# Layer 0's row maxima: turned in fp32, and split into three bfloat16 parts behind the turn on ScalarE and GpSimd instead of ahead of it on VectorE

## The chip, the cores and the metric

The kernel runs on one core of a Trainium2 chip, in one launch. The metric is device time in microseconds. The engines are called as the profile calls them: PE (TensorE matmul), PEld (TensorE weight load), DVE (VectorE), ACT (ScalarE), POOL (GpSimd) and SP (the queue that issues most DMAs). Each engine works through its own instructions in order and waits on semaphores for the others.

## The reference

Two layers work on an input of 2 x 1024 tokens with 256 features. Each normalises its input and adds the results of an attention and of a feed-forward network. Layer 0's attention, where the change lies, is causal, has 32 heads of 8 features and 8 key heads, and is computed in fp32:

```python
scores = jnp.einsum('bhqd,bhkd->bhqk', q, k_rep) / scale
scores = jnp.where((kpos > qpos)[None, None], -jnp.inf, scores)
attn = jax.nn.softmax(scores, axis=-1)
out = jnp.einsum('bhqk,bhkd->bhqd', attn, v_rep)
return out.transpose(0, 2, 1, 3).reshape(B, T, C) @ Wo + bo
```

Its feed-forward network has weights and activations rounded to float8; layer 1 has an attention with another reshape and a feed-forward network with ternary weights. They matter here only as neighbours on the same engines.

## The kernel before

**Tiles.** Layer 0's attention goes through 16 query tiles of 128 tokens, (batch, tile) = (0,0) to (0,7) and then (1,7) down to (1,0). Below they are called turns 0 to 15, since each has one turn of its maxima. Queries and keys are kept as three bfloat16 parts each, stacked along the partitions of the tiles qmain, qlast, kmain and klast, so that a sum of bfloat16 products gives scores of nearly fp32 accuracy.

**The maxima.** For a tile, max_unit (line 1000) computes the scores with the queries along the partitions from the first parts alone (L1012), adds the causal mask (L984), and DVE reduces them to the negated maximum over the keys (L1024) into the tile mx: 128 queries x 32 heads in fp32. For tiles with i > 3 the keys are taken in two halves, and take_max joins the two results by a minimum.

**The turn.** The exponentials are computed with the keys along the partitions and the queries along the free dimension, so -max can't be an activation's bias. It goes into the matmul: three extra rows of qlast hold -max as three bfloat16 parts, and the matching rows of klast hold ones. For this, take_max (line 1032) splits mx by four DVE instructions (L1039 to L1042): a cast, a subtraction, a cast and a subtraction. Three slots later turn_max (line 1045) transposes all three parts, 96 columns, in one bfloat16 transposition on PE (L1047). ACT copies the result from PSUM (L1049), a DMA writes it to DRAM (L1051), and two DMAs bring it into the rows of qlast (L1053).

**The weighing.** weigh (line 1071) computes scores of 128 keys x 4 heads x 128 queries by two matmuls each (L1076: s<-qmain, then s<-qlast, which adds the low parts and -max). ACT takes the exponential (L1086), POOL zeroes what the mask forbids on the diagonal (L1090), and gather (L1106) adds p times v into acc, one group of four p later. Scores and turned maxima share a PSUM pool of four buffers (ps_t); the maxima have three of their own (ps_s).

**The order.** PE's order is written by hand. A slot holds one pair of score tiles, some maxima of later tiles (at a rate that spreads their cost), and a piece of other work: the float8 feed-forward network (ffn0, L268 to L318), the ternary weights of layer 1 (on DVE L342 to L350, on POOL the four products L351 to L354, then a DMA L339), layer norms (L184 to L205), projections and the splitting of their results (L824 to L829), normalising and output (L1121 to L1150). A function handed to after(n, f) runs n slots later. A tile's weighing begins 10 slots after its maxima are done (6 for the first three). The order on the other engines is made by a scheduler when the program is built; it does not follow the source line by line, so that an added instruction can also move its neighbours.

**Queues.** The three DMAs of a turn stand on SP's queue among the loads of later queries (L936), keys (L894) and inputs (L62). POOL's queue holds the diagonal selects, additions into x (L281, L1149, L1150), the ternary products, and DMA issues of its own.

Of the kernel before, what the change touches and what calls it, by code (L numbers as in the profile page):

```python
# [10 lines left out]
F32 = mybir.dt.float32  # L11
BF = mybir.dt.bfloat16
# [4 lines left out]
ALU = mybir.AluOpType  # L17
# [3 lines left out]
P = 128  # L21
# [6 lines left out]
NH0, KV0, HD0 = 32, 8, 8  # L28
# [21 lines left out]
def two_layers(ctx: ExitStack, tc: tile.TileContext, a: dict, out: bass.AP):  # L50
    nc = tc.nc
# [16 lines left out]
    ident = cp.tile([P, P], F32, tag="ident", name="ident")  # L68
    make_identity(nc, ident)
    ident_bf = cp.tile([P, P], BF, tag="ident_bf", name="ident_bf")  # L70
# [4 lines left out]
    for name, op, fill, sign in (  # L75
# [3 lines left out]
        m = both[name] = zp.tile([P, 2, P], BF, tag=name, name=name)  # L79
        nc.gpsimd.memset(m, 0.0)  # L80
        for e in range(2):
            for t in range(2):
                part = m[HALF * e : HALF * e + HALF, t, :]
                nc.gpsimd.affine_select(
                    out=part,
                    in_=part,
# [705 lines left out]
    def attention0(w, qlast, tables):  # L792
# [11 lines left out]
        with ExitStack() as es:  # L804
            pool = es.enter_context(tc.tile_pool(name="a0", bufs=2))
            es.enter_context(tc.manual_schedule(engines={mybir.EngineType.PE}))
            dram = es.enter_context(tc.tile_pool(name="a0d", bufs=2, space=bass.MemoryType.DRAM))
            ps_s = es.enter_context(tc.tile_pool(name="a0s", bufs=3, space=PSUM))
            ps_t = es.enter_context(tc.tile_pool(name="a0t", bufs=4, space=PSUM))
# [155 lines left out]
            def after(slots, f):  # L965
                later.append((slot + slots, f))
# [65 lines left out]
            def take_max(b, i):  # L1032
                both = mx.pop((b, i))
                m = both[:, 0].rearrange("p e n -> p (e n)")
                parts = pool.tile([P, 3, NH0], BF, tag="mparts", name=f"mp{b}{i}", bufs=1)
                r = pool.tile([P, NH0], F32, tag="mrest", name=f"mr{b}{i}")
                if i > 3:
                    nc.vector.tensor_tensor(both[:, 0], both[:, 0], both[:, 1], ALU.min)
                nc.vector.tensor_copy(parts[:, 0], m)  # L1039
                nc.vector.tensor_tensor(r, m, parts[:, 0], ALU.subtract)  # L1040
                nc.vector.tensor_copy(parts[:, 1], r)
                nc.vector.tensor_tensor(parts[:, 2], r, parts[:, 1], ALU.subtract)  # L1042
                after(3, lambda: turn_max(b, i, parts))

            def turn_max(b, i, parts):
                ps = ps_t.tile([P, P], BF, tag="t", name=f"mt{b}{i}")
                nc.tensor.transpose(ps[: 3 * NH0], parts.rearrange("p a h -> p (a h)"), ident_bf)  # L1047
                mt = pool.tile([3 * NH0, P], BF, tag="mt", name=f"mts{b}{i}", bufs=2)
                nc.scalar.copy(mt, ps[: 3 * NH0])  # L1049
                scr = dram.tile([3 * NH0, P], BF, tag="mscr", name=f"mscr{b}{i}")  # L1050
                nc.sync.dma_start(out=scr, in_=mt)  # L1051
                for e in range(2):
                    nc.sync.dma_start(  # L1053
                        out=qst[b, i][1][HALF * e + AUG : HALF * e + AUG + 3],
                        in_=scr.rearrange("(a e n) t -> e a n t", a=3, e=2)[e],
                    )

            def max_units(b, i):

                if i > 3:  # L1060
                    for p in range(16):
                        yield 1024, lambda p=p: max_unit(b, i, [p], 0, 512, 1, False)
                lo = 512 * (i // 4)
                width = (i % 4 + 1) * P
                n = (4, 2, 1, 1)[i % 4]
                for p in range(0, 16, n):
                    yield 2 * n * width, lambda p=p: max_unit(b, i, list(range(p, p + n)), lo, width, 0, True)
                yield 0, lambda: take_max(b, i)
# [375 lines left out]
```

## Time and profile before

| | |
|---|---|
| three timed runs | 1151.48, 1151.53, 1152.94 us; median 1151.53 |
| the profiled execution | 1152.2 us, its span 1150.4 us |
| mean granted PE clock | 0.927 |
| layer 0 (from the chain's lines) | to about 770 us |
| L1024, all reductions to maxima | 608 instructions, 373.0 us of DVE |
| L1086, all exponentials of layer 0 | 576 instructions, 307.6 us of ACT |
| L1090, diagonal selects | 128 instructions, 83.0 us of POOL |
| the turns (L1047 on PE) | 16, from 64.2 to 738.9 us |

The profile shows one execution. In its lists of groups, a row is a line of the kernel, an engine, an operation, the tile written and those read, the shapes and the number of instructions; behind the bar stand the busy time in all and the mean duration of one in ns; behind a second bar, how long the engine was idle just before, and who ended that. In the timeline a row begins with its start and its length in us. In the chain of waits each piece is followed back to what released it; shares are of the span.

### The profile page before, as it was taken

The page shows a single profiled execution, that of the slowest core. Times are in us where ns is not written, and L with a number is a line of the kernel's source. Part 1 is how long each engine was busy: PE and PEld are TensorE (multiplying, and loading weights), DVE is VectorE, ACT ScalarE, POOL GpSimd, SP SyncE. Part 2 cuts the span into 40 slices and gives each one's busy share as a digit, 9 for nine tenths or more (in the row PEclk, how much of TensorE's full clock was granted, in tenths as well). Part 3 has the DMA queues.
Part 4 walks back from the last instruction along what each step waited for, and adds up shares of the span by engine and source line. Part 5 has one row for each costly group of instructions (what it writes and reads, how often), then busy time and mean ns, then how long its engine had stood idle before and what let it go on. Part 6 is the DMA issues. An engine that isn't in the chain of part 4 may idle for free.

```text
span 1150.4 us, 19967 instructions
## 1 busy us (share of the span) xinstructions
PE 1008.0 (88%) x7676; PEld 483.0 (42%) x7699; DVE 761.3 (66%) x1434; ACT 607.9 (53%) x1097; POOL 400.4 (35%) x440
## 2 busy tenths in 40 slices
PE   5858797897998989998989989987999999898897
PEld 2333332232432313232323333334567677576576
DVE  6567977889687898889796879413554544543531
ACT  3014571674455757688867766852564444433431
POOL 2007224324135121412123254554744535413400
PEclk9758896998899989999999999998899999989998
DMA  5432101101102010100010110008522332331100
GB/s 176 120 103 75 53 2 40 21 21 41 55 3 51 6 28 10 37 10 8 21 24 5 28 26 6 5 7 103 86 49 47 79 58 43 82 63 34 39 20 20
DMA packets 65927, 49.04 MB, mean 43 GB/s; under 512 B 20904, under 2 KB 59432, under 8 KB 65832
## 3 DMA queue, kind: packets, MB, share of 16 engines
q1 hardware_dynamic: 60632, 39.05, 15.0%
q0 software_dynamic: 4112, 8.26, 3.0%
q8 instruction: 60, 0.98, 0.4%
q10 hardware_dynamic: 1088, 0.46, 0.1%
q14 instruction: 35, 0.29, 0.1%
HBM read 34.12 MB, written 15.20 MB: 43 GB/s over the span
## 4 chain that ended last, share of the span: by engine, by line
PE 53%; DVE 25%; DMA 8%; ACT 6%; POOL 3%; issue 3%; SPq 2%; DVEq 0%; ACTq 0%; POOLq 0%
DVE mx L1024 13%; PE acc L1106 8%; PE s L1076 7%; PE f1gu L672 5%; PE sk L551 4%; PE f1o L711 3%; PE m L1012 3%; PE pqk L465 3%; PE sq L516 3%; DMA qscr<-ptq 2%; PE gu L301 2%; ACT p L1086 2%; DMA qs<-mscr 2%; SPq L936 2%; DMA qkv<-all 2%
## 5 line engine op out<-in xcount | busy, mean ns | idle before, releaser
L1024 DVE TENSOR_REDUCE mx<-m 128x1 f32<-128x512 f32 (+3 forms) x608 | 373.0, 653 | 99.8 <-PE m L1012 53.3
L1086 ACT ACTIVATE p<-s 128x512 f32<-128x512 f32 x576 | 307.6, 606 | 123.1 <-PE s L1076 119.1
L1106 PE MATMUL acc<-p,v 128*9 128x512 f32 x1152 | 170.4, 610 | 1.8 <-ACT p L1086 1.2
L1090 POOL TENSOR_SCALAR_AFFINE_SELECT p<-p 128x512 f32<-128x512 f32 x128 | 83.0, 673 | 152.6 <-ACT p L1086 152.4
L1012 PE MATMUL m<-k,qmain 64*128 64x512 bf16 (+3 forms) x384 | 95.1, 357 | 43.7 <-DVE mx L1024 34.4
L1012 PE MATMUL m<-kmain,qmain 64*128 64x512 bf16 (+3 forms) x384 | 81.7, 330 | 21.8 <-DVE mx L1024 19.9
L1012 PEld LDWEIGHTS <-qmain 64*128 64x128 bf16 x768 | 50.3, 98 | 80.9 <-issue 52.0
L984 PEld LDWEIGHTS <-ident_h 64*128 64x128 bf16 x832 | 45.7, 97 | 82.7 <-issue 59.8
L984 PE MATMUL m<-mask_q,ident_h 64*128 64x128 bf16 (+3 forms) x832 | 73.7, 221 | 1.8 <-DVE mx L1024 1.7
L1076 PE MATMUL s<-qmain,k 64*128 64x512 bf16 x288 | 65.7, 394 | 6.3 <-DVE att L1129 2.7
L1076 PE MATMUL s<-qmain,kmain 64*128 64x512 bf16 x288 | 65.3, 385 | 6.7 <-ACT p L1086 4.2
L1076 PE MATMUL s<-qlast,k 35*128 35x512 bf16 x288 | 62.8, 390 | 0.0
L1076 PE MATMUL s<-qlast,klast 35*128 35x512 bf16 x288 | 61.5, 381 | 0.0
L1076 PEld LDWEIGHTS <-k 64*128 64x128 bf16 (+1 forms) x576 | 21.0, 95 | 93.0 <-issue 84.5
L672 PEld LDWEIGHTS <-wgu_bf 128*128 128x128 bf16 x384 | 38.5, 101 | 42.4 <-issue 6.8
L681 DVE SCALAR_TENSOR_TENSOR h<-h,f1gu 128x512 f32<-128x512 f32 x32 | 22.0, 686 | 51.6 <-ACT h L680 51.6
L686 POOL TENSOR_TENSOR sq<-h 128x512 f32<-128x512 f32 x28 | 29.1, 1040 | 70.3 <-DVE h L682 67.5
L551 PE MATMUL sk<-qs,ks 25*128 25x128 f32 x512 | 45.3, 424 | 7.7 <-DMA qs<-mscr 7.6
L1149 POOL TENSOR_TENSOR x<-x,aos 128x256 f32<-128x256 f32 x16 | 12.6, 788 | 112.6 <-ACT aos L1148 112.6
L559 ACT ACTIVATE p<-sk 128x2048 f32<-128x2048 f32 x16 | 30.0, 1878 | 41.0 <-PE sk L551 41.0
L524 DVE TENSOR_REDUCE m<-sq 128x16 f32<-128x2048 f32 x16 | 36.6, 2287 | 21.8 <-PE sq L516 21.7
L154 POOL TENSOR_TENSOR hp<-hrest,hp 128x512 bf16<-128x512 f32 x32 | 37.0, 1157 | 34.8 <-ACT hp L153 34.8
(288 smaller groups left out, 1803.1 us busy)
## 6 DMA issues: line engine op xcount, KB each, us to landing
qmain<-qscr SPq DMA_DIRECT2D x64, 96.0 KB
qkv<-all SPq DMA_DIRECT2D x16, 384.0 KB
qscr<-ptq POOLq DMA_DIRECT2D x6, 384.0 KB, 4.2
x<-in_x SPq DMA_DIRECT2D x16, 128.0 KB
qmain<-qscr SPq DMA_DIRECT2D x32, 64.0 KB
qs<-qkv SPq DMA_DIRECT2D x16, 128.0 KB
ks<-qkv SPq DMA_DIRECT2D x16, 128.0 KB
vs<-qkv SPq DMA_DIRECT2D x16, 128.0 KB
```

Source lines behind the costliest of these rows:

```text
L154: engines[1].tensor_tensor(parts[2], r, parts[1], ALU.subtract)
L465: nc.tensor.matmul(pqk, x[k], wqk[:, k, :], start=(k == 0), stop=(k == 1))
L524: last(nc.vector.tensor_reduce(m, ps, AX.X, ALU.max, negate=True))
L551: nc.tensor.matmul(ps[:, s, r, :], columns(k, slice(S * s, S * s + HD + 9), 4 * b + r), columns(q, slice(S * s, S * s + HD + 9), 4 * b + r ...
L672: nc.tensor.matmul(ps[g], wgu_bf[:, k, g * HID + hc * P : g * HID + (hc + 1) * P], x_parts[n][m][:, k, :], start=(k == 0 and m == 0), stop ...
L984: nc.tensor.matmul(out[e][:, :, lo:], ident_h[rows, t, :], rhs.to_broadcast([HALF, out[e].shape[1], P - lo]), start=start and t == 0, stop ...
L1012: nc.tensor.matmul(sc[e][:, s * width : (s + 1) * width], qst[b, i][0][rows, p, :], kst[b][0][rows, lo // 512, p // 4, 0:width], start=not ...
L1024: reduced = nc.vector.tensor_reduce(mx[b, i][:, part, e, pairs[0] : pairs[0] + n], sc[e][:, : n * width].rearrange("p (s k) -> p s k", s=n ...
L1076: nc.tensor.matmul(sc[e], kst[b][n][rows, j // 4, u, j % 4 * P : (j % 4 + 1) * P], qst[b, i][n][rows, 4 * u : 4 * u + 4, :], start=n == 0, ...
L1086: nc.scalar.activation(p, sc[e], AF.Exp, scale=scale)
L1090: nc.gpsimd.affine_select(out=by_head, in_=by_head, compare_op=ALU.is_ge, fill=0.0, base=0, pattern=[[0, 4], [1, P]], channel_multiplier=-1,)
L1106: nc.tensor.matmul(acc[32 * s : 32 * s + HD0 + 1, :], vst[b][:, j, 4 * G + s, :], ps[s], start=(j == 0), stop=(j == i),)
```

## The change

take_max keeps the fp32 maxima and no longer splits them; for i > 3 it still joins the two halves on DVE. turn_max transposes the 32 fp32 columns on PE into an fp32 PSUM tile. Behind it ACT copies the result twice from PSUM, once as bfloat16 (the first part) and once as fp32; POOL subtracts the one from the other; ACT casts the rest to bfloat16 (the second part); POOL subtracts again and writes the third part. Then come the same three DMAs, of a tile of 32 partitions x 3 x 128 instead of 96 partitions x 128. The tile mt has one buffer where it had two, and the new tiles turned and rest have one each.

```diff
             def take_max(b, i):
                 both = mx.pop((b, i))
                 m = both[:, 0].rearrange("p e n -> p (e n)")
-                parts = pool.tile([P, 3, NH0], BF, tag="mparts", name=f"mp{b}{i}", bufs=1)
-                r = pool.tile([P, NH0], F32, tag="mrest", name=f"mr{b}{i}")
                 if i > 3:
                     nc.vector.tensor_tensor(both[:, 0], both[:, 0], both[:, 1], ALU.min)
-                nc.vector.tensor_copy(parts[:, 0], m)
-                nc.vector.tensor_tensor(r, m, parts[:, 0], ALU.subtract)
-                nc.vector.tensor_copy(parts[:, 1], r)
-                nc.vector.tensor_tensor(parts[:, 2], r, parts[:, 1], ALU.subtract)
-                after(3, lambda: turn_max(b, i, parts))
-
-            def turn_max(b, i, parts):
-                ps = ps_t.tile([P, P], BF, tag="t", name=f"mt{b}{i}")
-                nc.tensor.transpose(ps[: 3 * NH0], parts.rearrange("p a h -> p (a h)"), ident_bf)
-                mt = pool.tile([3 * NH0, P], BF, tag="mt", name=f"mts{b}{i}", bufs=2)
-                nc.scalar.copy(mt, ps[: 3 * NH0])
-                scr = dram.tile([3 * NH0, P], BF, tag="mscr", name=f"mscr{b}{i}")
-                nc.sync.dma_start(out=scr, in_=mt)
+                after(3, lambda: turn_max(b, i, m))
+
+            def turn_max(b, i, m):
+
+                ps = ps_t.tile([P, P], F32, tag="t", name=f"mt{b}{i}")
+                nc.tensor.transpose(ps[:NH0], m, ident)
+                turned, rest = (
+                    pool.tile([NH0, P], F32, tag=f"m{x}", name=f"m{x}{b}{i}", bufs=1) for x in ("turned", "rest")
+                )
+                mt = pool.tile([NH0, 3, P], BF, tag="mt", name=f"mts{b}{i}", bufs=1)
+                nc.scalar.copy(mt[:, 0], ps[:NH0])
+                nc.scalar.copy(turned, ps[:NH0])
+                nc.gpsimd.tensor_tensor(rest, turned, mt[:, 0], ALU.subtract)
+                nc.scalar.copy(mt[:, 1], rest)
+                nc.gpsimd.tensor_tensor(mt[:, 2], rest, mt[:, 1], ALU.subtract)
+                scr = dram.tile([3, NH0, P], BF, tag="mscr", name=f"mscr{b}{i}")
+                nc.sync.dma_start(out=scr.rearrange("a n t -> n a t"), in_=mt)
                 for e in range(2):
                     nc.sync.dma_start(
                         out=qst[b, i][1][HALF * e + AUG : HALF * e + AUG + 3],
-                        in_=scr.rearrange("(a e n) t -> e a n t", a=3, e=2)[e],
+                        in_=scr[:, 16 * e : 16 * e + 16],
                     )
```

In the new kernel the transposition is L1042, the three copies are L1047, L1048 and L1050, the two subtractions L1049 and L1051, and the DMAs L1053 and L1055.

As the programs are built, PE's order is the same but for the transposition. DVE has 64 rows fewer, ACT 32 more and POOL 32 more. On ACT the first two copies stand where the one copy stood. What stands between the second and the third copy on ACT, and just ahead of the first subtraction on POOL, is, by the lines of the kernel before:

| turn | on ACT between second and third copy | on POOL ahead of the first subtraction |
|---|---|---|
| 1 | L824 | L864 |
| 3 | two L1086 | L352 |
| 4 | L1115 | L351 |
| 5 | L824 | L864 |
| 6 | three L1086 | L353 |
| 7, 8, 15 | one L1086 | L1090; L354; L1150 |
| 9 | nothing | L351 |
| 10 | L313 | L1090 |
| 13 | L1115 | L1150 |
| 14 | one L198 | L354 |
| 0, 2, 11, 12 | nothing | L242; L1090 in 2, 11 and 12 |

In turn 1 POOL's second diagonal select comes behind L829 where it came ahead of it; in turns 3 and 7 some selects come behind ternary products; in turn 5 two exponentials come ahead of the cast L828 on ACT, and L829 comes behind L353 on POOL.

## Prediction

> **What bounds the kernel now.** I read the page first, then the table by stage, the groups by form, the chain of waits in order of time, and last the timeline around each of the 16 places where a maximum is turned. The profiled execution took 1152.2 us (span 1150.4 us and 1.8 us around it); the three timed runs have a median of 1151.53 us. My sum is made against 1152.2 and moved by -0.67 at the end.
>
> ```profile
> PE 1008.0 (88%) x7676; PEld 483.0 (42%) x7699; DVE 761.3 (66%) x1434; ACT 607.9 (53%) x1097; POOL 400.4 (35%) x440
> ...
> PE 53%; DVE 25%; DMA 8%; ACT 6%; POOL 3%; issue 3%; SPq 2%; DVEq 0%; ACTq 0%; POOLq 0%
> ```
>
> The first line says that PE is the busiest; the second, of the chain that ended last, that a quarter of the span hangs on DVE and little on ACT or POOL. By stage, 100 to 700 us has DVE busy 38 to 45 us of each 50 and PE 41 to 47, ACT 18 to 43, POOL 9 to 20: there layer 0's maxima (L1024) and scores take turns as the bound.
>
> ```profile
> L1049 ACT COPY mts<-mt 96x128 bf16<-96x128 bf16 x16 | 4.2, 265 | 5.8 <-PE mt L1047 5.8
> L1047 PE MATMUL mt<-ident_bf,mp 128*96 128x128 bf16 x16 | 4.0, 250 | 1.5 <-ACT p L1086 0.9 <-DVE v L957 0.6
> L1039 DVE CAST mp<-mx 128x32 bf16<-128x32 f32 x16 | 3.3, 206 | 0.1
> L1041 DVE CAST mp<-mr 128x32 bf16<-128x32 f32 x16 | 3.2, 201 | 0.2
> L1042 DVE TENSOR_TENSOR mp<-mr,mp 128x32 bf16<-128x32 f32 x16 | 3.2, 201 | 0.2
> L1040 DVE TENSOR_TENSOR mr<-mx,mp 128x32 f32<-128x32 f32 x16 | 2.9, 183 | 0.2
> ```
>
> These are all the rows that the change takes away: after the bar, busy us in all and mean ns of one.
>
> **What DVE gains.** 206 + 201 + 201 + 183 = 791 ns a turn, 12.7 us in all, but not all of it is on the path. The chain in order of time holds 3.9 us of these four lines (turns 2, 3, 4, 5, 10, 11, 12, 13). Two of its pieces:
>
> ```profile
> 161.20 0.63 DVE mp L1039
> ...
> 162.89 0.10 DVE mr L1040
> ```
>
> I count **-3.9**. The remaining 8.8 us stand beside PE work and I take them as nothing; if DVE is second in line in those places too, up to that much more could come off.
>
> **What ACT and POOL get.** One copy of 265 ns becomes three, of 32x128. The trace has none of that shape; 128 elements a partition took 265 ns here, 128x256 took 371 ns (L1148), a 128x4 activation 0.21 us: I take 0.26, the row with the same free size, so +0.52 us a turn. The two POOL subtractions, 32x128, stand between a 128x8 iota (154 ns) and 128x256 (672 ns, L281); the straight line through 672 and 1157 ns (128x512, L825) gives 0.43 us, which I take. Handing on from ACT to POOL and back costs 0.08 and 0.03 us (at 271.83 and 271.18 us). So a turn's parts take at least 0.52 + 0.08 + 0.43 + 0.03 + 0.26 + 0.08 + 0.43, about 1.8 us instead of 0.26, on two queues that others share.
>
> The new wait is the price: **the third copy (L1050 of the new kernel) waits on ACT for POOL's first subtraction, and the exponentials behind it wait too.** The order of the built programs tells what stands ahead of that subtraction on POOL. In turns 2, 3, 7, 10, 11 and 12 POOL is free, or ACT has a gap behind the copy (1.76 us at 131.05, 22.4 us at 195.41, 1.68 us at 671.48): nothing. In four turns POOL is in the middle of a ternary weight's L351 to L354. Turn 8:
>
> ```profile
> 473.39 1.16 POOL L351 TENSOR_TENSOR tmg<-tmg,tlg 128x512 bf16<-128x512 bf16 x1 [2.06 <-DVE tlg L350]
> ...
> 474.06 0.26 ACT L1049 COPY mts<-mt 96x128 bf16<-96x128 bf16 x1
> ...
> 475.03 2.07 ACT L1086 ACTIVATE p<-s 128x512 f32<-128x512 f32 x4 [0.70 <-PE s L1076]
> ...
> 477.28 1.05 PE L1106 MATMUL acc<-p,v 128*9 128x512 f32 x8
> 478.11 1.15 POOL L354 TENSOR_TENSOR wgu_bf<-tmg,twg 128x512 bf16<-128x512 bf16 x1
> ```
>
> The new order has the subtraction behind L354, which ends at 479.26; the third copy stands behind the first of the four exponentials. It can run at 479.7, so the second exponential starts at 479.9 instead of 475.53, the gather (477.28) gets its last operand at 480.5 and PE goes on at 480.9 instead of 478.25: **+2.7**. By the same reading:
> - Turn 6: the subtraction stands behind L353, which ends at 350.77. The fourth exponential moves from 346.92 to 351.4; PE's next scores, which waited for ACT until 350.40 anyway, come at 352.7: **+2.3**.
> - Turn 14: behind L354 (ends 728.04); exponentials from 727.12 to 729.2, the gather at 728.81 waits 1.4: **+1.4**.
> - Turn 4: behind L351 (ends 218.65); the copy stands behind L1115, the exponential at 216.99 moves by 1.4 to 2 us, but scores and gather need it only at 219.4: **+0.3**.
> - Turn 9: behind L351 (ends 532.55); the first normalised row moves from 532.61 to 533.25; L351 itself waits for DVE, which is earlier: **+0.4**.
>
> Two turns change by order alone. In turn 1 the second diagonal select (ends 106.12) is put behind the 1.2 to 2.15 us of L829; the gather at 104.07 waits for it and PE resumes about **+1.5** later. In turn 5 the cast L828, for which ACT waited 1.55 us, comes behind two exponentials, and the gather that waited 1.23 us for them goes earlier: **-0.7**, since DVE is busy right behind.
>
> The rest: turns 10, 13 and 15 delay one exponential by 0.4 to 1.2 us, partly in ACT's gaps, and the longer copies count where ACT is on the chain: **+0.8**. PE's transposition in fp32 lies between the bfloat16 one (250 ns) and 128x128 f32 (285 ns, L1121; 295, L1137): +0.05 a turn on a chain that is half PE: **+0.4**.
>
> **The result's way to its use** is hidden. POOL's second subtraction has L825 ahead of it in turn 1, L353 in turns 3 and 4, the DMA issue L339 in 6 and 8; so its DMA (L1051) goes out later by 2.4 us in turn 1, 7.7 in 3, 8.4 in 6, 6.3 in 8 and 1.4 to 6 in the others, and SP's loads of later queries (L936, wanted a tile later) with it. From the old second issue of L1053 to the first use of that tile (L1076 on qlast) there are 5.5 us in turns 0 and 1 and 9 to 25 in the others; quiet DMAs take 1.4 us (216.09 to 217.51). The closest are turn 1 (1.7 us left after that and the landing) and turn 8 (3.8): if this cover fails, each us late there is a us of the whole. The DMA still moves 96 runs of 256 bytes. The single buffers cost nothing: two turns are never closer than 15 us (725.10 to 740.08), a DMA takes 1.4. The PSUM tile is held one copy longer, 0.26 us.
>
> Sum: -3.9 - 0.7 + 2.7 + 2.3 + 1.4 + 0.3 + 0.4 + 1.5 + 0.8 + 0.4 = **+5.2 us**: 1157.4 on the profiled execution's scale, 1156.7 on the median's.
>
> **A rule against the change.** DVE's L216 took 3.00 us at 280.45 against 614 ns in the mean while POOL ran selects, and casts of 128x32 took up to 711 ns against a median of 172: work on POOL can hold DVE. The Trainium skill, page "GPSIMD Engine Reference", section "Key points", says why: POOL shares SBUF interfaces with VectorE, and DVE instructions in a two-port mode or with two SBUF inputs contend. If each new subtraction held DVE for its 0.43 us, 32 of them would cost 13.8 us of DVE time and eat the 12.7; my sum has nothing for it, and by that rule in full it would be up to 3.9 us higher (the gain gone). In the same page's section "Engine selection" POOL is called about twice as slow in two-input work; from 183 ns that makes 0.37 us, as an estimate, and moves no term by more than 0.1.
>
> **Rivals.**
> - *Faster: the stalls don't reach the end.* ACT is idle almost half of the time, and PE has maxima to do while it waits. If only the small terms (0.8, 0.4 and 0.3) remain, the sum is -4.6 + 1.5 = -3.1: 1148.4; with half of the 8.8 us of hidden DVE work in addition, 1144.0. It decides from the point where the blocks in turns 6, 8, 14 and 1 cost less than 2.7 us together. For it speaks that DVE is 25% of the chain and ACT 6%; against it that the gathers at 477.28 and 348.28 need the very exponentials that are blocked.
> - *No change that shows* (a run-to-run difference of 0.2%, 2.3 us, is about what can be told from nothing): half of the blocks absorbed, +5.2 - 4.0 = +1.2: 1152.7.
> - *Much slower: the late result is waited for, or POOL holds DVE.* Turn 1 and 8 late by 2 us each, or the 3.9 us of gain lost: +9 to +13, 1160.5 to 1164.5.
> - *That the change does not do what it says* is excluded by the order of the built programs: 64 rows fewer on DVE, 32 more each on ACT and POOL.
>
> **Numbers.** The forecast's case (+2.3 to +8) has 0.46, much slower 0.12, no change 0.17, faster 0.25. So faster 0.25, same 0.17, slower 0.58. The range leaves out the lower end of faster and the far end of much slower, 1145.5 to 1164.5.
>
> **What would show it.** Right: ACT idle before the third copy's line with POOL as the releaser, 4 us in turns 6 and 8 and about 2 in 4 and 14; PE's gather waiting for ACT there; DVE busy 12 us less; POOL 14 us and ACT 8 us more; layer 1 as long as before. Wrong: the third copy starting right behind its neighbours, a wait of PE's scores for the DMA into qlast, or mean durations of L1024 that rise above 653 ns.

## The result, and the profile after

The changed kernel took 1162.21 us (median of six runs, 1157.88 to 1163.41) against 1151.51 us (six runs, 1149.64 to 1154.04): a ratio of 1.0082, 95% interval 1.0059 to 1.0104. It is slower, by about twice the forecast's 5.2 us (9.4 us by the ratio, 10.7 by the medians). That is above the forecast's own case of +2.3 to +8 and inside the rival "much slower" (1160.5 to 1164.5), which had been given a chance of 0.12. The profiled execution, at 1158.51 us, was one of the two fastest of the six, so its span shows only 6.4 us of the loss. Layer 0 shows more: the first matmul that reads the last turn's qlast came at 770.0 us, 13.4 us later than before, and layer 1 gave about 7 us back under a mean granted clock of 0.95 instead of 0.93 behind 770 us. In a second profiled run of the changed kernel (g0 below, span 1160.9 us) the clock there was 0.93 as in the kernel before, and the loss in layer 0 stayed: from the transposition of turn 0 to that of turn 15 both runs of the changed kernel took 686.0 us, the kernel before 674.7. So the profile is read for layer 0, and the size is taken from the timed runs.

From the page of the changed kernel: busy time by engine, and the reductions.

```profile
PE 1008.4 (87%) x7699; PEld 480.0 (41%) x7699; DVE 756.8 (65%) x1370; ACT 614.0 (53%) x1129; POOL 414.1 (36%) x472
...
L1024 DVE TENSOR_REDUCE mx<-m 128x1 f32<-128x512 f32 (+3 forms) x608 | 371.8, 653 | 114.2 <-PE m L1012 67.5
```

POOL has 13.7 us more and ACT 6.1 (forecast: 14 and 8); DVE has only 4.5 us less, where 12 were forecast. L1024 still takes 653 ns. The shares of the chain that ended last hardly moved (POOL from 3% to 4%, DMA from 8% to 7%): a loss of 1% doesn't show in them.

The groups by form of the changed kernel, for the rows that replace the six shown of before:

```profile
L1049 POOL TENSOR_TENSOR mrest<-mturned,mts 32x128 f32<-32x128 f32 x16 | 9.0, 561 | 61.2 <-ACT mturned L1048 61.0
L1051 POOL TENSOR_TENSOR mts<-mrest,mts 32x128 bf16<-32x128 f32 x16 | 8.4, 524 | 2.1 <-ACT mts L1050 2.0
L1050 ACT CAST mts<-mrest 32x128 bf16<-32x128 f32 x16 | 4.8, 297 | 22.0 <-POOL mrest L1049 22.0
L1042 PE MATMUL mt<-ident,mx 128*32 128x128 f32 x16 | 4.7, 296 | 1.6 <-ACT p L1088 0.9 <-DVE v L957 0.6
L1048 ACT COPY mturned<-mt 32x128 f32<-32x128 f32 x16 | 4.1, 254 | 0.0
L1047 ACT CAST mts<-mt 32x128 bf16<-32x128 f32 x16 | 3.9, 245 | 5.9 <-PE mt L1042 5.9
```

The prices are near the estimates: copies 245 to 297 ns (0.26 us), subtractions with a median of 0.42 and 0.43 us (0.43), the transposition 296 ns (at most 295). What costs is in the last column: the third copy (L1050) kept ACT idle for 22.0 us, and POOL was the releaser. The timeline shows where that reaches PE, in turns 6, 8 and 14 (start, length, instruction, idle time ahead of it):

```profile
351.17 0.30 ACT L1050 CAST mts<-mrest 32x128 bf16<-32x128 f32 x1 [4.15 <-POOL mrest L1049]
...
352.01 1.03 PE L1108 MATMUL acc<-p,v 128*9 128x512 f32 x2 [2.70 <-ACT p L1088]
...
482.83 0.30 ACT L1050 CAST mts<-mrest 32x128 bf16<-32x128 f32 x1 [3.94 <-POOL mrest L1049]
...
483.67 1.71 PE L1108 MATMUL acc<-p,v 128*9 128x512 f32 x2 [2.09 <-ACT p L1088]
...
739.53 0.37 PE L1078 MATMUL s<-qmain,kmain 64*128 64x512 bf16 x1 [1.98 <-ACT p L1088]
```

This is the mechanism of the forecast, in its place, and the waits have the size that was forecast: in turns 6 and 8 ACT stands for 4.15 and 3.94 us, the next exponential is late, and PE's gather waits 2.70 and 2.09 us for it. ACT's waits in turns 4 and 14 are 2.08 and 2.22 us (forecast: about 2). In turn 14 it is the scores (L1078) that wait for an exponential, 1.98 us, and not the gather, as the forecast had it.

What these waits cost shows in PE's lag: how much later the same matmul starts than in the trace of the kernel before. It grows by 2.8 us in turn 6, 4.5 in turn 8 and 3.8 in turn 14 (forecast: 2.3, 2.7 and 1.4). In turns 8 and 14 that is more than the wait, in part because PE runs slower behind it (last section).

Turn 1 holds what the forecast had left at zero. The timelines of PE, DVE and POOL there, in the changed kernel:

```profile
107.71 1.03 PE L1108 MATMUL acc<-p,v 128*9 128x512 f32 x2 [1.00 <-POOL p L1092]
109.42 1.03 PE L1108 MATMUL acc<-p,v 128*9 128x512 f32 x2 [0.68 <-POOL p L1092]
...
105.67 1.12 DVE L216 TENSOR_SCALAR few<-spare_last 128x1024 int32<-128x1024 int32 x1
...
107.17 3.41 DVE L219 TENSOR_SCALAR few<-few 128x1024 f32<-128x1024 f32 x1
...
105.08 1.16 POOL L825 TENSOR_TENSOR restk<-k01y,ptk 128x512 f32<-128x512 f32 x1 [0.19 <-ACT ptk L824]
106.19 0.87 POOL L1051 TENSOR_TENSOR mts<-mrest,mts 32x128 bf16<-32x128 f32 x1
107.03 0.63 POOL L1092 TENSOR_SCALAR_AFFINE_SELECT p<-p 128x512 f32<-128x512 f32 x1
107.63 1.14 POOL L829 TENSOR_TENSOR ptk<-restk,ptk 128x512 bf16<-128x512 f32 x1
108.74 0.62 POOL L1092 TENSOR_SCALAR_AFFINE_SELECT p<-p 128x512 f32<-128x512 f32 x1
109.32 0.77 POOL L879 DMA_DIRECT2D kscr<-ptk  x1
```

The gather's two waits for late selects, 1.7 us together, are the forecast's +1.5. But L219 took 3.41 us on DVE, where the same instruction took 0.68 us before. It began while POOL was busy, POOL went from one instruction to the next without a gap, and L219 ended at 110.58, 0.68 us behind 109.90. If its work took its usual 0.68 us, it ran when POOL had come to its DMA issue; the row doesn't tell waiting from work, so this is inferred. All reductions behind it, and PE behind them, were late. Between 105 and 113 us of the kernel before, PE's lag grew from 1.2 to 5.5 us; from just ahead of the turn to just behind it, it grew by 2.8.

Not every such DVE instruction is held that long: just ahead, L216 also began behind a busy POOL (L825), and it was through in 1.12 us, while POOL's next instruction, L1051, took 0.87 us instead of its median of 0.43. It was let in between the two.

In turn 5 the same thing works for the change. The first row is the kernel before, the second the changed one:

```profile
280.45 3.00 DVE L216 TENSOR_SCALAR fe<-fw 128x1024 uint16<-128x1024 uint16 x1
...
283.30 0.58 DVE L216 TENSOR_SCALAR fe<-fw 128x1024 uint16<-128x1024 uint16 x1
```

The long L216, which the prediction named as its sign that POOL can hold DVE, is gone beside the new order of POOL's work, and PE's lag falls by 2.4 us at this place, in both profiled runs of the changed kernel. The forecast had -0.7 for the whole turn, from another cause.

### The profile page after: what moved, and what is told of

Read it like the earlier page. It is cut to its first block, busy times and chain, and to the rows that moved or that the text cites. A ratio compares the mean times of both kernels' runs of the same rounds, so it can differ in the third digit from the quotient of the medians.

```text
span 1156.8 us, 19991 instructions
## 1 busy us (share of the span) xinstructions
PE 1008.4 (87%) x7699; PEld 480.0 (41%) x7699; DVE 756.8 (65%) x1370; ACT 614.0 (53%) x1129; POOL 414.1 (36%) x472
## 4 chain that ended last, share of the span: by engine, by line
PE 53%; DVE 25%; DMA 7%; ACT 6%; POOL 4%; issue 3%; SPq 2%; DVEq 0%; ACTq 0%; POOLq 0%
DVE mx L1024 13%; PE acc L1108 8%; PE s L1078 7%; PE f1gu L672 5%; PE sk L551 4%; PE m L1012 4%; PE f1o L711 3%; PE pqk L465 3%; PE sq L516 3%; DMA qscr<-ptq 2%; ACT p L1088 2%; PE gu L301 2%; DMA qs<-mscr 2%; PE m L984 2%; DMA qkv<-all 1%
## 5 line engine op out<-in xcount | busy, mean ns | idle before, releaser
L1024 DVE TENSOR_REDUCE mx<-m 128x1 f32<-128x512 f32 (+3 forms) x608 | 371.8, 653 | 114.2 <-PE m L1012 67.5
L1108 PE MATMUL acc<-p,v 128*9 128x512 f32 x1152 | 174.9, 622 | 6.9 <-ACT p L1088 4.8
L1078 PE MATMUL s<-qmain,kmain 64*128 64x512 bf16 x288 | 66.2, 390 | 9.0 <-ACT p L1088 6.2
L1078 PE MATMUL s<-qmain,k 64*128 64x512 bf16 x288 | 65.8, 401 | 3.4 <-ACT p L1088 1.3
L1078 PE MATMUL s<-qlast,k 35*128 35x512 bf16 x288 | 62.9, 396 | 0.0
L1078 PE MATMUL s<-qlast,klast 35*128 35x512 bf16 x288 | 62.2, 385 | 0.0
L1078 PEld LDWEIGHTS <-k 64*128 64x128 bf16 (+1 forms) x576 | 20.8, 96 | 91.1 <-issue 84.4
```

The lines of the kernel that those rows point to most:

```text
L1024: reduced = nc.vector.tensor_reduce(mx[b, i][:, part, e, pairs[0] : pairs[0] + n], sc[e][:, : n * width].rearrange("p (s k) -> p s k", s=n ...
L1078: nc.tensor.matmul(sc[e], kst[b][n][rows, j // 4, u, j % 4 * P : (j % 4 + 1) * P], qst[b, i][n][rows, 4 * u : 4 * u + 4, :], start=n == 0, ...
L1108: nc.tensor.matmul(acc[32 * s : 32 * s + HD0 + 1, :], vst[b][:, j, 4 * G + s, :], ps[s], start=(j == 0), stop=(j == i),)
```

## The experiments

The first four ask whether ACT's wait is the cause. At that time it was the whole theory, with the two rivals "POOL holds DVE" and "the late result is waited for".

**e1, no wait.**

```diff
-                nc.scalar.copy(mt[:, 1], rest)
+                nc.scalar.copy(mt[:, 1].rearrange("p (a b) -> p a b", a=2), groups[:NH0, None, 64:].to_broadcast([NH0, 2, 64]))
```

> The third copy casts zeros instead of the rest: the second part is zero and the third holds the whole rest in bfloat16 (the computation is changed in that alone). Each engine has the work of the changed kernel, but ACT no longer waits for POOL, and as the program is built, turn 1's second diagonal select stands ahead of L829 again. Theory (ACT's queue stands behind POOL): the blocks in turns 6, 8, 10, 14 and turn 1's 3 to 4 us go, about 13 us of layer 0 in all, and what is left is the gain on DVE and the longer copies: 1149 us (1146 to 1151.5), a ratio of 0.996 to 1.000 to the kernel before. Rival (POOL's subtractions hold DVE): they are all still there, so 1158 or more. Rival (the late result is waited for): the third part still goes out at the end of POOL's chain, so 1158 or more.

Measured: 1.0076 (1.0048 to 1.0104), no better than the changed kernel. Its timeline says why, and that it was no clean test:

```profile
105.16 4.89 DVE L216 TENSOR_SCALAR few<-spare_last 128x1024 int32<-128x1024 int32 x1
...
492.13 0.30 ACT L1050 COPY mts<-groups 32x128 bf16<-32x128 bf16 x1 [4.32 <-DMA mscr<-mts]
```

A copy that needs nothing was put far ahead, into the turn before its own. There it waits for the DMA that empties the single buffer mt, so that ACT stands again, for 4.32 us in turn 8 and for 20.0 us in eight places together. The wait that I meant to remove had come back in another form. And in turn 1 an instruction of DVE (L216, 0.83 us before) took 4.89 us. The run rules out neither theory, but it pointed at turn 1.

**e2, the first part alone**: DVE loses its work and nobody gets it.

```diff
-                nc.scalar.copy(turned, ps[:NH0])
-                nc.gpsimd.tensor_tensor(rest, turned, mt[:, 0], ALU.subtract)
-                nc.scalar.copy(mt[:, 1], rest)
-                nc.gpsimd.tensor_tensor(mt[:, 2], rest, mt[:, 1], ALU.subtract)
```

(mt is one of two tiles that are zeroed once.)

> Only the first part is made, by one copy on ACT behind the fp32 turn; the second and third parts are zeros (left out: the splitting of -max; everything else and the three DMAs stay). DVE has lost its four instructions a turn and nothing has been put elsewhere, so this is the gain alone, with the fp32 transposition. Theory of the forecast: 3.9 us and a little more come off, less 0.4 for PE: 1147.5 us (1145 to 1150). If all 12.7 us of DVE were on the path: 1139. If DVE's work there was hidden: 1151 to 1152.

Measured: 0.9938 (0.9916 to 0.9960), so 7.1 us less on the scale of 1151.5. From its page:

```profile
PE 1006.2 (88%) x7676; PEld 481.4 (42%) x7699; DVE 753.6 (66%) x1370; ACT 608.1 (53%) x1097; POOL 400.8 (35%) x442
```

DVE is busy 7.7 us less, not 12.7. The durations of DVE's instructions overlap, as the timeline of the kernel before shows (turn 8):

```profile
469.12 0.68 DVE L1024 TENSOR_REDUCE mx<-m 128x1 f32<-128x512 f32 x1
469.73 0.17 DVE L1039 CAST mp<-mx 128x32 bf16<-128x32 f32 x1
469.81 0.68 DVE L1024 TENSOR_REDUCE mx<-m 128x1 f32<-128x512 f32 x1
```

L1039 lasts 0.17 us, but the next instruction starts 0.08 us behind its start. So the 64 instructions were worth about 7.7 us of DVE. The timed runs are 7.1 us shorter (4.6 to 9.7 by the interval), where I had counted 3.9 less 0.4. But the trace of e2 doesn't show that gain where the instructions stood: from turn 0 to turn 15 it took 674.0 us against 674.7 before, at a granted clock of 0.92 against 0.93, and 3.7 us came off behind turn 15 (407.8 against 411.5), at 0.95 against 0.94. So how much of the 7.1 us is DVE's work on the path, and how much the clock, was not separated.

**e3, the subtractions on DVE**, behind the turn.

```diff
-                nc.gpsimd.tensor_tensor(rest, turned, mt[:, 0], ALU.subtract)
+                nc.vector.tensor_tensor(rest, turned, mt[:, 0], ALU.subtract)
                 nc.scalar.copy(mt[:, 1], rest)
-                nc.gpsimd.tensor_tensor(mt[:, 2], rest, mt[:, 1], ALU.subtract)
+                nc.vector.tensor_tensor(mt[:, 2], rest, mt[:, 1], ALU.subtract)
```

> The changed kernel with both subtractions on DVE instead of POOL, behind the turn; the three copies stay on ACT, and ACT now waits for DVE. Theory (a late answer blocks ACT's queue): DVE's queue is full of reductions of 0.65 us and ternary pieces of 0.7 to 0.9 us, shorter than POOL's products of 1.2 us, so ACT's wait falls from 22 us over 14 turns to about 8, and half of DVE's gain is gone; 1152 to 1157. Rival (POOL holds DVE): POOL has no work of the turns any more, so no loss is left and half of the gain stays: 1148 to 1151.

Measured: 1.0022 (1.0005 to 1.0039). From its list of waits (in all, times, longest):

```profile
ACT mts L1050 <- DVE mrest L1049: 9.8, 8, 2.7
```

ACT's wait fell from 22.0 to 9.8 us, as expected, and the time lies between the theory's ends. In turn 1 L216 and L219 took 0.67 and 1.17 us. The run fits both causes and decides nothing between them.

**e4, the cast on POOL**: the one change that takes ACT's wait away cleanly.

```diff
-                nc.scalar.copy(mt[:, 1], rest)
+                nc.gpsimd.tensor_copy(mt[:, 1], rest)
```

> The changed kernel with one instruction moved: the cast to the second part is POOL's, not ACT's, so that POOL does subtraction, cast, subtraction and nothing on ACT waits for POOL. Nothing is left out. Theory (ACT's queue stands behind POOL): as without the wait, 1149 us (1146 to 1152); POOL busy about 6 us more. Rival (POOL holds DVE): 16 instructions more on POOL, so 1160 or more. Rival (late result): POOL's chain is no shorter, so 1158 or more, and PE's scores wait for the DMA into qlast.

Measured: 1.0043 (1.0022 to 1.0064), between theory and rival. ACT waits for POOL nowhere in its list of waits, and the loss in turns 6, 8 and 14 is gone from its trace: PE's lag grows there by 0.0, 0.1 and 0.4 us. This is the cleanest evidence for ACT's wait, since POOL and DVE kept all their work of the changed kernel and POOL got the cast in addition. But turn 1 is as bad as in e1:

```profile
105.12 4.62 DVE L216 TENSOR_SCALAR few<-spare_last 128x1024 int32<-128x1024 int32 x1
```

In this run and in e1 the selects stand ahead of L829 again, as before the change; so it isn't their order that holds DVE. My theory, ACT's wait alone, fell here. The next one has two causes: ACT's wait in turns 6, 8 and 14, and DVE held in turn 1.

**f1, turn 1 as before**, and the other 15 turns as changed (the old functions are kept beside the new for the turns in a list).

```diff
+                if (b, i) in AHEAD:  # [(0, 1)]
+                    nc.vector.tensor_copy(parts[:, 0], m)
+                    nc.vector.tensor_tensor(r, m, parts[:, 0], ALU.subtract)
+                    nc.vector.tensor_copy(parts[:, 1], r)
+                    nc.vector.tensor_tensor(parts[:, 2], r, parts[:, 1], ALU.subtract)
+                    after(3, lambda: turn_parts(b, i, parts))
+                    return
```

> The changed kernel, but turn 1 alone is done as in the kernel before: four instructions on DVE ahead of a bfloat16 turn, one copy on ACT, nothing on POOL; the other 15 turns are the changed kernel's. Theory now (two causes: in turn 1 POOL's longer unbroken run holds one DVE instruction, 3.41 us instead of 0.68 for L219, and the reductions and PE behind it lose 4 us; in turns 6, 8, 10 and 14 ACT waits for POOL): only the first goes, so the ratio to the kernel before falls from 1.0082 to 1.004 to 1.0055 (1156 to 1159 us). If turn 1's loss is only where the new order shows up and is made good later: no difference to 1.008. If the whole loss were POOL holding DVE: about 1.000.

Measured: 1.0029 (1.0009 to 1.0050), a little better than the theory's range. Turn 1 alone was worth 0.53% or 6.1 us (1.0082 less 1.0029, uncertain by some 0.3%). From its timelines:

```profile
105.08 0.68 DVE L219 TENSOR_SCALAR few<-few 128x1024 f32<-128x1024 f32 x1
...
106.14 1.21 DVE L221 TENSOR_TENSOR fsw<-spare_last,few 128x1024 f32<-128x1024 f32 x1
...
106.22 2.15 POOL L829 TENSOR_TENSOR ptk<-restk,ptk 128x512 bf16<-128x512 f32 x1
...
479.73 1.02 PE L1132 MATMUL acc<-p,v 128*9 128x512 f32 x2 [2.09 <-ACT p L1112]
```

L219 is at 0.68 us again, and POOL is the one that waits, as in the kernel before: L829, which takes 1.14 us by itself, took 2.15 beside L221, which had started 0.08 us ahead of it. PE's lag doesn't grow in turn 1, so POOL's delay costs less here than DVE's. In the traces turn 1 is worth less than in the times: 3.4 us from turn 0 to turn 15 (682.6 against 686.0). The wait of turn 8 is still there, 2.09 us to the digit.

**f2, both at once.**

```diff
+                if (b, i) in AHEAD:  # [(0, 1)]
...
-                nc.scalar.copy(mt[:, 1], rest)
+                nc.gpsimd.tensor_copy(mt[:, 1], rest)
```

> Both at once: turn 1 as in the kernel before, and in the other 15 turns the cast to the second part on POOL instead of ACT, so that ACT waits for POOL nowhere. Theory now (turn 1's hold of DVE and ACT's waits are the two causes, about 4 us each): the loss is gone and most of the gain on DVE shows: ratio 0.995 to 1.000 (1146 to 1151.5 us on the scale of the kernel before at 1151.5). Rival (POOL's instructions hold DVE in every turn by a little): 48 instructions less three on POOL still cost, 1.002 or more.

Measured: 1.0011 (0.9989 to 1.0033): the value misses the theory's range (0.995 to 1.000), and the interval covers the range's upper end and the lower end of the rival's. In its trace neither cause is left, but against the kernel before PE falls back by 1 to 3 us each in turns 4, 5 and 10, partly for a while only, where DVE's L224, L315 and L316 took 1.85, 2.63 and 1.52 us (0.69, 0.42 and 0.69 in the median). Such long ones occur in the kernel before as well (L216, 3.00 us), and L224 takes 1.85 us in the changed kernel too, so this is an indication only.

**e6, two slots later**: the third copy, the second subtraction and the DMAs.

```diff
+                def second():
                     nc.scalar.copy(mt[:, 1], rest)
                     nc.gpsimd.tensor_tensor(mt[:, 2], rest, mt[:, 1], ALU.subtract)
...
+                after(2, second)
```

> The changed kernel with the third copy, the second subtraction and the DMAs two slots later in the program's order, so that other work of ACT stands ahead of the third copy while POOL gets done. Nothing is left out. Theory now: ACT's wait for POOL falls from 22 us over 14 turns to below 8; if turn 1 still holds DVE, the ratio is 1.002 to 1.005. Rival (late result): the parts reach qlast some 4 us later in each turn, cover is 5.5 us less a landing of 1.4 us in turns 0 and 1, so a wait of PE for the DMA shows there and the ratio is 1.008 or more.

Measured: 1.0062 (1.0038 to 1.0086). ACT's wait fell only to 18.3 us where I had expected less than 8, and the ratio lies between the theory and the rival. The rival's wait is real:

```profile
120.96 0.77 PE L1082 MATMUL s<-qlast,k 35*128 35x512 bf16 x2 [4.55 <-DMA qlast<-mscr]
```

In turn 1 PE waited 4.55 us for the DMA into qlast; no DVE instruction was held there (L216 1.11 us, L219 0.68). The changed kernel's list of waits has no such wait: the forecast's 1.7 us of cover held there, and two slots more would use it up.

**e7, only more work on POOL**, in the kernel before.

```diff
                 nc.scalar.copy(mt, ps[: 3 * NH0])
+                spare = pool.tile([NH0, P], F32, tag="spare", name=f"sp{b}{i}", bufs=1)
+                nc.gpsimd.tensor_tensor(spare, mt[:NH0], mt[:NH0], ALU.subtract)
+                nc.gpsimd.tensor_tensor(spare, mt[:NH0], mt[:NH0], ALU.subtract)
```

> The kernel before, with two subtractions of 32x128 added on POOL behind every turn's copy, whose result nobody reads (so they add work and take none away). ACT and DVE have the work of before, and ACT waits for POOL nowhere new. Theory now: POOL's added work costs only where its unbroken run meets a DVE instruction of the kind it holds, which is in turn 1 if the built order puts them between L864 and L825 there: 2 to 5 us (1.002 to 1.004), by a single DVE instruction of 3 us or more between 104 and 110 us. If POOL's work were free: 1.000. If every subtraction held DVE by its own 0.43 us: DVE busy 14 us more, 1.006 or more.

Measured: 1.0044 (1.0017 to 1.0070). The place was not the one that I named. In turn 1 L216 and L219 took 1.17 and 0.68 us. The long one came in turn 5:

```profile
271.94 4.47 DVE L315 TENSOR_SCALAR fw<-fw 128x1024 bf16<-128x1024 bf16 x1
...
274.97 1.14 POOL L352 TENSOR_TENSOR tmg<-tmg,tsg 128x512 bf16<-128x512 bf16 x1
276.07 0.82 POOL L879 DMA_DIRECT2D kscr<-ptk  x1
```

L315 takes 0.41 us by itself and ended at 276.41: by the same reckoning it ran when POOL had come to its first DMA issue, behind four instructions (L825 to L352) without a gap. In return L216, 3.00 us in turn 5 of the kernel before, took 0.41 here. So work on POOL that nobody waits for costs time, and a held DVE instruction is how the trace shows it; which one it would be, the built order had not told me.

**g0, the changed kernel again.** No edit.

> The changed kernel itself once more, to have it beside the others on one chip: 1.0082 as in the result, within its interval of 1.0059 to 1.0104; the third copy waits for POOL some 22 us in 14 turns, and one DVE instruction of turn 1 (L216 or L219) takes 3 us or more. If the length of that one instruction were chance, it would be below 1.5 us here and the time 3 us shorter.

Measured: 1.0085 (1.0060 to 1.0110). L219 took 3.41 us again, ACT's wait was 22.0 us in 14 turns again, and the gather of turn 8 waited 2.09 us. So it is not the chance of one execution.

**g1, turns 1, 6, 8 and 14 as before**, twelve as changed.

```diff
-            AHEAD = [(0, 1)]
+            AHEAD = [(0, 1), (0, 6), (1, 7), (1, 1)]
```

> The changed kernel with turns 1, 6, 8 and 14 done as in the kernel before (four instructions on DVE ahead of a bfloat16 turn), the other 12 turns as in the changed kernel: the three turns in which ACT's wait reached PE in the traces, and the one in which DVE is held. Theory now: against turn 1 alone (1.0029) the ACT waits of turns 6, 8 and 14, some 2 to 4 us each in that run's trace, go too: 0.996 to 1.000. If ACT's waits cost nothing at the end: 1.002 to 1.004 as with turn 1 alone.

Measured: 0.9943 (0.9920 to 0.9965), **faster than both kernels**, by 6.6 us against the one before. The gather's group in f1 and then in g1 (idle time behind the second bar):

```profile
L1132 PE MATMUL acc<-p,v 128*9 128x512 f32 x1152 | 173.4, 618 | 5.9 <-ACT p L1112 4.8 <-POOL p L1116 0.8 <-ACT o L1141 0.2
```

```profile
L1132 PE MATMUL acc<-p,v 128*9 128x512 f32 x1152 | 170.2, 613 | 1.1 <-POOL p L1116 0.8 <-ACT o L1141 0.2
```

With three turns less in the new form, the gather no longer waits for ACT at all. 0.86% or 9.9 us came off, so ACT's waits in turns 6, 8 and 14 were the larger of the two causes. The traces agree: from turn 0 to turn 15 g1 took 673.5 us against f1's 682.6, and PE's lag grows in turns 6, 8 and 14 by 0.0, 0.3 and 1.4 us against 2.8, 3.2 and 3.8. ACT still waits 11.6 us in other turns, 5.0 of them in one; those reach no gather.

**g2, another mix**: turns 1, 4, 5 and 10 as before, and POOL's cast in the rest.

```diff
-            AHEAD = [(0, 1)]
+            AHEAD = [(0, 1), (0, 4), (0, 5), (1, 5)]
```

> A try for a faster version: turns 1, 4, 5 and 10 as in the kernel before, and in the other 12 turns the changed kernel with the cast to the second part on POOL. These are the four turns in which PE still lost 1 to 3 us each against the kernel before in the trace of the run with POOL's cast and turn 1 as before (1.0011). Theory now: what those turns lost is gone and 12 turns of DVE relief stay: 0.994 to 0.999. If the losses only move to other DVE instructions: 1.000 or more.

Measured: 1.0003 (0.9975 to 1.0030). Not faster; the expectation failed. In its trace PE stays within 3 us of the kernel before through all of layer 0: the losses of those turns are gone, but so is the gain of turn 5, where L216 took 2.99 us again.

**g3, the splitting on POOL ahead of the turn.**

```diff
-                nc.vector.tensor_copy(parts[:, 0], m)
-                nc.vector.tensor_tensor(r, m, parts[:, 0], ALU.subtract)
-                nc.vector.tensor_copy(parts[:, 1], r)
-                nc.vector.tensor_tensor(parts[:, 2], r, parts[:, 1], ALU.subtract)
+                nc.gpsimd.tensor_copy(parts[:, 0], m)
+                nc.gpsimd.tensor_tensor(r, m, parts[:, 0], ALU.subtract)
+                nc.gpsimd.tensor_copy(parts[:, 1], r)
+                nc.gpsimd.tensor_tensor(parts[:, 2], r, parts[:, 1], ALU.subtract)
```

> The kernel before with its four splitting instructions (128x32) on POOL instead of DVE, still ahead of the bfloat16 turn; ACT has its one copy as before. Theory: nothing new waits on ACT, but 64 instructions run on POOL, and PE's transposition now waits for POOL three slots later. From 0.42 us for 32x128, a 128x32 form with a quarter of the elements a partition takes POOL between 0.1 and 0.42 us, so 0.4 to 1.7 us a turn: if POOL's queue is clear, the gain on DVE alone (0.994); if PE's transposition waits for POOL behind ternary products, or the unbroken run holds DVE, 1.000 to 1.008. I expect 0.997 to 1.003.

Measured: 0.9980 (0.9963 to 0.9997), a little faster than before. Three slots of lead hide POOL's time, and ACT has nothing to wait for. No DVE instruction of turn 1 was held (L216 1.11 us, L219 0.68).

## Why the prediction was right in sign and short in size

Four ratios to the kernel before split the loss. Each kernel differs from the next by the turns named, and a difference of two is uncertain by some 0.3%, 3.5 us.

| from, to | what comes in | share | us, by the times | forecast |
|---|---|---|---|---|
| before, e2 | DVE's work goes, fp32 transposition comes | -0.62% | -7.1 | -3.9 + 0.4 |
| e2, g1 | the new work in 12 turns; 4 turns keep DVE's | +0.05% | +0.6 | +0.8 (rest), +0.3, +0.4, -0.7 |
| g1, f1 | turns 6, 8 and 14 in the new form | +0.86% | +9.9 | +2.3, +2.7, +1.4 |
| f1, after | turn 1 in the new form | +0.53% | +6.1 | +1.5 |
| sum | | +0.82% | +9.4 | +5.2 |

- **DVE's gain: probably larger than counted.** "I count -3.9" took only what the chain showed. e2's timed runs gave 7.1 us, its trace 0.7 us between turns 0 and 15. The prediction itself allowed for more where DVE is second in line; no run here shows that this happened. The 12.7 us, as a sum of overlapping durations, were too many: DVE had about 7.7.
- **ACT behind POOL: right**, in its turns, releaser and waits (4.15, 3.94, 2.08 and 2.22 us for 4, 4, 2 and 2; the gather's 2.70 and 2.09 for about 2.3 and 2.7). At the end the three turns cost 9.9 us instead of 6.4, and the lags say where: 4.5 instead of 2.7 in turn 8 (3.2 in f1) and 3.8 instead of 1.4 in turn 14. The forecast had no term for PE's clock behind a wait. In turn 14 PE waited 1.98 us and ran at 0.50 for some 2 us behind it, in three executions; in turn 8 the lag grew by 4.5 and 4.6 us where the clock fell and by 3.2 where it didn't.
- **Turn 1: the step that failed.** The late selects were there as forecast (1.7 us). The rest is the rule that the prediction weighed and then left out: "my sum has nothing for it". It had been priced as 0.43 us on each of 32 subtractions. It came as one instruction held for 3.41 us; the turn cost 6.1 us by the times and 3.4 by the traces of f1 and the changed kernel.
- **Turn 5: a gain that the prediction didn't see.** Its -0.7 came from the order on ACT. The lag fell by 2.4 us where the held L216 of the kernel before was let go. So POOL's hold on DVE was left out on both sides, and turn 5 hid part of what turn 1 cost.
- **POOL holds DVE** was a rival's half. The prediction's sign that would have shown it, a mean of L1024 above 653 ns, was the wrong one: L1024's mean stayed at 653 to 655 ns in every run, and the long ones were the conversions between them. The Trainium skill, page "SBUF — State Buffer", section "Who interferes with whom", says that tensor_scalar can enter a two-port mode in which it competes with POOL for one pair of ports, that tensor_tensor with both inputs in SBUF competes with POOL's reads, that a tensor_reduce doesn't on trn2, and that whoever issues first has the pair for its whole instruction. The runs agree on who is held and on the first coming (L829's 2.15 us in f1), but they also show more than one instruction's length: 3.41, 4.62, 4.89 and 4.47 us behind a row of POOL's.
- **The late result: hidden, as forecast**; e6 shows how near it was.
- **DVE 12 us less** came as 4.5: about 7.7 by the count above and 2.4 from L216 in turn 5, less 2.7 given back by L219 in turn 1 and the rest by other long instructions.
- **Luck** had a part in the sign and the size: the stalls, turn 1 among them, cost more than forecast, DVE's work (by the times) and turn 5 gave more, and the errors went against each other. The sum of the rival "faster", -3.1, also leaves out one of the two terms of +0.4; with it the sum is -2.7.
- **Layer 1 as long as before**: not in the profiled execution (7 us back), for the granted clock; in g0 within 1 us.

Why POOL's cast with turn 1 as before (f2, 1.0011) doesn't come down to g1's 0.9943, though its gather waits for ACT as little, the traces tell in part. Between 200 and 300 us of the kernel before, in turns 4 and 5, f2's lag grows by 2.6 us while g1's falls by 3.8; at the end of layer 0 f2 is 6.6 us behind g1. In f2 PE waits 3.23 us for DVE in turn 4 (att, behind L224), and L315 takes 2.63 us in turn 5; g1 has the changed kernel's order there and its gain. g2 took those turns back to the old form and with it the long L216. What stays open is what decides, from one built order to the next, which DVE instruction is held and for how long, and how much of e2's gain is DVE's.

## What to carry to other kernels

Taking work off DVE, the engine with a quarter of the chain here, was worth 7.1 us by the times. What such a change costs is decided where its answer is waited for: a chain that goes from ACT to POOL and back stops everything behind the second ACT instruction, for as long as POOL's longest queue. It was best here to keep the old form in the few turns whose wait reaches the bound; four of sixteen turned 0.8% of loss into 0.6% of gain. And before anything is added to POOL, find the stretches in which POOL runs without a gap beside DVE conversions from SBUF to SBUF, because the price can come there in one piece, and because a new order can remove such a hold as well as make one.

## What the runs showed of the hardware

- A DVE conversion that starts behind a busy POOL can be held over several of POOL's instructions: in the changed kernel, e1, e4 and e7 for 3.41 to 4.89 us, ending when POOL had come to a DMA issue (L879). The same instruction took 3.41 us in two executions. It isn't always so: L216 in turn 1 of the changed kernel was let in behind one instruction (1.12 us), and f2's L315 (2.63 us, from 275.88) ended at 278.51, when POOL had gone from L351 to L352 without a DMA issue. What decides was not found.
- After the wait of turn 8 PE ran slower for some 4 us. A window of the changed kernel (from, to, length, busy time and instructions of PE, PEld, DVE, ACT and POOL, granted clock, DMA share, GB/s):

```profile
484.00:488.00 4.00, 4.00 (x16) 0.88 (x15) 1.19 (x2) 2.63 (x7) 1.34 (x2) 0.59 0.27 45
```

  The granted clock was 0.59 there (0.98 in the 4 us ahead), and two matmuls s<-qmain took 0.61 us instead of 0.39. g0 showed 0.65 in its window from 480 to 484 us, in which its wait ends. But in f1 the same wait of 2.09 us was followed by 1.00, and so was the longer one of turn 6 in the changed kernel (2.70 us). Behind the wait of turn 14 (1.98, 1.98 and 1.97 us) the clock was 0.50 for 2 us in the changed kernel (741 to 743 us), g0 (738 to 740) and f1 (736 to 738), and 1.00 there in the kernel before. So a wait can cost more than its length, and it doesn't always.
